# A four-layer graph network: layer 1's row vector spread by one transfer, and the buffers divided anew

## The chip, the cores and the metric

The kernel runs on one core of a Trainium2 chip. Its engines are TensorE (PE, with its weight loads shown apart as PEld), VectorE (DVE), ScalarE (ACT), GpSimd (POOL) and SyncE (SP), which here only issues transfers. The metric is device time in microseconds of the whole program; less is better. A line number such as L911 is a line of the kernel before the change.

## The reference

There are 32 independent graphs of 512 nodes with 256 features, each with a dense 512 x 512 adjacency matrix, all in 32-bit floats. Four layers follow each other, each with a residual and a layer norm:

```
x = norm(x + MLP(adj @ x + (1 + eps) x))            # layer 0, hidden 512
x = norm(x + GAT(x, adj > 0.5))                     # layer 1, 4 heads of 64
x = norm(x + MHA(x, log(adj + 1e-6)))               # layer 2, 8 heads of 32
x = norm(x + softmax(mask((x W) x^T * adj)) x)      # layer 3
```

The change touches layer 1. There the score of the pair (i, j) in head h is leaky_relu(dst[i, h] + src[j, h]) with slope 0.2, masked by adj > 0.5, and goes through a softmax over j.

## The kernel before

The graphs are not worked off one after another. The function `graph` describes all work of one graph as named steps, each with an engine, a cost in microseconds, the steps that it follows, and the buffers that it takes. `Plan.order` then simulates all engines with these costs and writes the instructions of all graphs in the order in which its simulation started them. Up to six graphs are open at once (the `window`), so that layers of different graphs overlap. Each engine works off its instructions in that order; the planner's times decide the order alone, and the real engines wait on semaphores. The tuple given to `plan.run` holds the due time between graphs (33.0), how far ahead of the earliest candidate it may look (0.0), the window, the price put on a change of TensorE's tiling mode (55.0), and seeds that move the due times of some steps at random; a search over seeds is what "annealed" means.

`transfer(name, us, after, queue)` stands for a transfer that was issued: `us` on a modelled queue, which works off its entries one at a time, and then a fixed 2.0 us until it has landed.

Memory is divided in classes. "B" are large buffers of 8 KB a partition (a 512 x 512 matrix), "C" those of 4 KB, and "D" strips of 2 KB (128 x 512). A take such as `D=A00/8` needs more than 8 free ones of the class. Strips hold the adjacency rows A0 of layer 0 and A3 of layer 3, ATd, layer 3's z3 and eT, the nodes' masks, and some rows of layers 1 and 2. Large buffers hold the transposed adjacency AT, h1T, layer 1's four z and layer 2's E chunks.

Layer 1 writes the exponential of the leaky score as a product, so that most of it needs no exponential of a matrix. The row vector R holds, for each of the four heads, exp(0.8 src[j]) over the 512 nodes; S and T hold factors that depend on i or j alone by partition. One activation (L911) makes Relu(S R - T) for 128 x 512 pairs, and VectorE (L922) adds T and multiplies by the edge mask. For L911 a head's R, one row of 512, must stand in all 128 partitions. It is made as columns, transposed by TensorE (step Rt, L853), copied to SBUF as rows of 128 (Re, L858), stored to a scratch tensor in device memory (Rsi, L863), and read back with one row spread over all partitions (Rl0 to Rl3, L872), one head after the other. Two more rows, the sums xs of the features over all nodes, go the same way: they are spread into the strip xsr (hsbi, L880), and VectorE multiplies them by the weights into hs (hsl, L888), a bias needed by layer 1's output copy (L959). GpSimd issues transfers that add while they move: the biases onto x (L583), and sums of z (L974 in layer 1, L1149 in layer 2), on a queue of their own.

Of the kernel before, what the change touches and what calls it, by code (L numbers as in the profile page):

```python
# [10 lines left out]
F32 = mybir.dt.float32  # L11
I32 = mybir.dt.int32
U8 = mybir.dt.uint8
AF = mybir.ActivationFunctionType
# [3 lines left out]
P = 128  # L18
# [6 lines left out]
H1 = 4  # L25
# [5 lines left out]
def row_bcast(ap, n):  # L31

    return bass.AP(tensor=ap.tensor, offset=ap.offset, ap=[[0, P], [1, n]])
# [13 lines left out]
class Plan:  # L47
# [30 lines left out]
    def step(self, name, eng, us, after=(), take=(), free=(), mode=""):  # L78


        def add(emit):
            steps = self.steps[-1]
            known = {**steps, **{f"^{n}": s for n, s in self.steps[0].items()}}
            assert name not in steps and all(a in known for a in after), (name, after)
            takes = []
            for b in take:
                kind, _, key = b.partition("=")
                key, _, rest = key.partition("/")
                takes.append((kind, key or kind, int(rest or 0)))
            steps[name] = Step(eng, us, dict.fromkeys(after), takes, mode, emit)  # L90
            for b in free:
                self.free(b, (name,))
            return emit

        return add
# [129 lines left out]
def fast_path(  # L225
# [23 lines left out]
    nc = tc.nc  # L249
    B, N, D = x.shape  # L250
    NC = N // P
    DC = D // P
# [10 lines left out]
    dram = ctx.enter_context(tc.tile_pool(name="dram", bufs=3, space=bass.MemoryType.DRAM))  # L263
# [33 lines left out]
    def blk(i):  # L297
# [1 line left out]


    plan = Plan({
        "B": 11, "C": 12, "D": 19, "p": 8,

        "live": 6, "L0": 1, "L1": 2, "L2": 2, "L3": 1, "AT": 4, "zs": 7, "edge": 1, "tmp": 2,
    })
    step = plan.step

    def prev(name, i):

        return (f"{name}{i-1}",) if i else ()  # L310

    def row(name, n):
        return tuple(f"{name}{i}" for i in range(n))

    def transfer(name, us, after, queue="q1"):


        @step(f"{name}.q", queue, us, after)
        def _():
            pass  # L320

        @step(name, None, 2.0, (f"{name}.q",))
        def _():
            pass
# [231 lines left out]
    def graph(g):  # L556
# [3 lines left out]
        t = {"g": g}  # L560

        def big(key, shape, name):
            return sb.tile(shape, F32, tag=f"B{slot[key]}", name=f"{name}_{g}")
# [4 lines left out]
        def strip(key, shape, name):  # L568
            return sb.tile(shape, F32, tag=f"D{slot[key]}", name=f"{name}_{g}")
# [88 lines left out]
        for c in range(NC):  # L658

            @step(  # L660
                f"la{c}i", "sp", 0.45, (f"la{c-1}i",) if c else (),
                take=(f"D=A0{c}/5",) if c else ("live", "L0", "D=A00/8"),
            )
            def _(c=c):
                t[f"A{c}"] = strip(f"A0{c}", [P, N], f"A{c}")
                nc.sync.dma_start(t[f"A{c}"], adj[g].rearrange("(c p) m -> p c m", p=P)[:, c, :])
# [192 lines left out]

        @step("Rsi", "sp", 0.45, ("Re",))  # L860
        def _():
            t["Rdram"] = dram.tile([H1 * NC + DC, P], F32, tag="R_dram", name=f"R_dram_{g}")
            nc.sync.dma_start(t["Rdram"], t["Rr"])  # L863

        transfer("Rs", 0.2, ("Rsi",))

        for h in range(H1):

            @step(f"Rl{h}i", "sp", 0.45, ("Rs",) + ((f"Rl{h-1}i",) if h else ()), take=(f"D=R{h}/4",))
            def _(h=h):  # L870
                t[f"R{h}"] = strip(f"R{h}", [P, N], f"R_bc_{h}")
                nc.sync.dma_start(t[f"R{h}"], row_bcast(t["Rdram"][h * NC : (h + 1) * NC, :], N))  # L872

            transfer(f"Rl{h}", 0.8, (f"Rl{h}i",))


        @step("hsbi", "sp", 0.45, ("Rs",), take=("D=xsr/3",))
        def _():
            t["xsr"] = strip("xsr", [P, 2, D], "xs_row")
            nc.sync.dma_start(t["xsr"][:, 0, :], row_bcast(t["Rdram"][H1 * NC :, :], D))  # L880

        transfer("hsb", 0.4, ("hsbi",))

        @step("hsl", "dve", 0.7, ("hsb", "^weg"), free=("xsr",))
        def _():
# [18 lines left out]
        for h in range(H1):  # L904
            for c in range(NC):

                @step(f"z{h}{c}", "act", 0.7, (f"Rl{h}", "ST") + prev(f"z{h}", c), take=() if c else (f"B=z{h}",))
                def _(h=h, c=c):
                    if c == 0:
                        t[f"e{h}"] = big(f"z{h}", [P, NC, N], f"z1_{h}")  # L910
                    nc.scalar.activation(  # L911
                        t[f"e{h}"][:, c, :], t[f"R{h}"], AF.Relu,
                        bias=t["nT"][:, h, c : c + 1], scale=t["S"][:, h, c : c + 1],
                    )

            for k in range(2):

                @step(f"zm{h}{k}", "dve", 1.32, (f"z{h}{2*k+1}",) + row("ed", NC))
                def _(h=h, k=k):
                    for c in (2 * k, 2 * k + 1):  # L920
                        z = t[f"e{h}"][:, c, :]
                        nc.vector.scalar_tensor_tensor(  # L922
                            z, z, t["T"][:, h, c : c + 1], t["edge"][:, c, :], op0=ALU.add, op1=ALU.mult
                        )

        plan.free("edge", tuple(f"zm{h}{k}" for h in range(H1) for k in range(2)))
        for h in range(H1):
            plan.free(f"R{h}", row(f"z{h}", NC))


        for hp in range(H1 // 2):
# [484 lines left out]
    for g in range(B):  # L1416
        graph(g)
    with tc.manual_schedule():
        plan.run([(33, 0.0, 6, 55.0, ((619770, 10.0), (518002, 10.0), (122525, 2.0), (401816, 5.0), (736052, 5.0), (898543, 5.0), (151957, 2.0), (89616, 2.0), (541939, 5.0), (120127, 10.0), (238703, 2.0), (316405, 2.0), (831071, 5.0), (164665, 2.0)), (0.7, 0.0, 0.0))])

# [427 lines left out]
@with_exitstack  # L1850
def four_layer_graph_kernel(ctx: ExitStack, tc: tile.TileContext, *args):
    flags = ctx.enter_context(tc.tile_pool(name="flags", bufs=1))
    beyond = flags.tile([1, 1], I32, name="beyond")
    fast_path(tc, *args, beyond)
    taken = tc.nc.values_load(beyond, min_val=0, max_val=1,
                              skip_runtime_bounds_check_because="is_lt gives 0 or 1")
    with tc.If(taken > 0):
        general_path(tc, *args)
# [34 lines left out]
```

## Time and profile before

| | |
|---|---|
| time, median of 3 | 3014.51 us (3012.42 to 3014.51) |
| span of the profiled run | 3008.2 us |
| granted TensorE clock | 0.996 |
| R_bc<-R_dram | 128 transfers of 256 KB |
| xs_row<-R_dram | 32 transfers of 128 KB |
| R_dram<-R_rows | 32 transfers of 9 KB |
| DMA queue q0 (GpSimd's) | 346.06 MB, 60.4% of 16 engines' span |
| DMA queue q1 (SyncE's) | 149.75 MB, 15.5% of 16 engines' span |

An engine's busy share is over the whole span. The matmuls are pipelined, so TensorE's busy time can contain lost time. A wait in square brackets at the end of a line of the order of time is idle time ahead of that instruction and what ended it. In the chain that ended last, each piece is what the next one waited for.

### The profile page before, as it was taken

To read this page: it belongs to the slowest core of one execution; us is meant where nothing else is said; L and a number is where in the kernel's file an instruction comes from. 1 tells how busy PE (TensorE), PEld (TensorE's weight loads), DVE (VectorE), ACT (ScalarE), POOL (GpSimd) and SP (SyncE) were. 2 spreads that over 40 slices of the span, in tenths; PEclk is the share of its full clock that TensorE was granted. 3 is DMA by queue.
4 is the path that set the end of the run, shared out by engine and by line. 5 is a ranking of instruction groups with operands and counts; after the bars stand their busy time and mean duration, and the time that the engine had idled before them with its cause. 6 is when DMAs were issued, how large, how long until landed. Compare 5 with 4: busy or idle time off the path is not lost.

```text
span 3008.2 us, 42752 instructions
## 1 busy us (share of the span) xinstructions
PE 2938.5 (98%) x15521; PEld 1687.7 (56%) x15521; DVE 2060.2 (68%) x4133; ACT 1928.2 (64%) x3818; POOL 626.8 (21%) x688
## 2 busy tenths in 40 slices
PE   8999999999999999999999999999999999999998
PEld 6546565565555565655656556555556565565544
DVE  3567767667667677676676766766767767667776
ACT  4666766666666667566676666665666766657664
POOL 1222212222122221222211222212222212222120
PEclk9999999999999999999999999999999999999999
DMA  6887787787787787877878777778778787786770
GB/s 175 179 173 171 166 188 161 167 177 156 173 176 168 164 173 166 191 159 160 182 149 192 163 167 175 163 167 186 164 165 168 163 191 157 166 179 143 163 171 15
DMA packets 180320, 498.89 MB, mean 166 GB/s; under 512 B 17980, under 2 KB 57736, under 8 KB 156296
## 3 DMA queue, kind: packets, MB, share of 16 engines
q0 software_dynamic: 77472, 346.06, 60.4%
q1 hardware_dynamic: 101648, 149.75, 15.5%
q8 instruction: 125, 2.05, 0.3%
q14 instruction: 91, 0.75, 0.1%
q10 hardware_dynamic: 984, 0.28, 0.0%
HBM read 183.25 MB, written 17.08 MB: 67 GB/s over the span
## 4 chain that ended last, share of the span: by engine, by line
PE 73%; DVE 10%; DMA 9%; ACT 5%; issue 2%; POOL 1%; SPq 0%; ACTq 0%; POOLq 0%; DVEq 0%
PE s L1317 8%; PE o_ps L1174 7%; PE s L1116 7%; PE y_ps L766 7%; PE o_ps L946 6%; DVE z L922 5%; PE o_ps L1371 5%; PE iT_ps L1303 4%; PE h1T_ps L747 4%; PE v_ps L815 4%; PE o2p_ps L1259 4%; ACT z L911 4%; PE v_ps L1097 4%; DMA xs_row<-R_dram 3%; DMA R_bc<-R_dram 3%; PE qT_ps L1079 2%
## 5 line engine op out<-in xcount | busy, mean ns | idle before, releaser
L1138 DVE SCALAR_TENSOR_TENSOR z<-AT,z 128x1024 f32<-128x1024 f32 x512 | 616.3, 1219 | 214.4 <-ACT z L1129 210.2
L1129 ACT ACTIVATE z<-s 128x512 f32<-128x512 f32 x1024 | 566.1, 602 | 126.9 <-PE s L1116 123.0
L911 ACT ACTIVATE z<-R_bc,nT,S 128x512 f32<-128x512 f32 x512 | 380.0, 809 | 181.7 <-DMA R_bc<-R_dram 181.6
L637 ACT ACTIVATE x<-x,shift,rstd 128x256 f32<-128x256 f32 x508 | 283.2, 592 | 127.9 <-DVE shift L627 127.8
L922 DVE SCALAR_TENSOR_TENSOR z<-z,T,edge 128x512 f32<-128x512 f32 x512 | 350.4, 746 | 10.7 <-ACT z L911 10.2
L1149 POOL DMA_DIRECT2D z<-z x186 | 165.9, 901 | 787.5 <-DVE z L1138 337.6
L1116 PE MATMUL s<-qT,kT 32*128 32x512 f32 x2048 | 313.3, 638 | 2.1 <-ACT qT L1085 2.1
L619 POOL TENSOR_TENSOR rstd<-ve,nhalf 128x4 f32<-128x4 f32 (+1 forms) x131 | 161.3, 1232 | 682.9 <-DVE ve L613 634.3
L974 POOL DMA_DIRECT2D z<-z x256 | 226.4, 953 | 300.1 <-DMA z<-z 183.4
L747 PE MATMUL h1T_ps<-hT,w_sb 128*128 128x512 f32 x512 | 243.0, 599 | 23.2 <-ACT hT L731 22.9
L946 PE MATMUL o_ps<-z,v 128*64 128x512 f32 x1024 | 244.9, 608 | 17.4 <-ACT z L1129 13.0
L1174 PE MATMUL o_ps<-z,v 128*32 128x512 f32 x2048 | 257.6, 600 | 3.8 <-DVE z L1138 3.8
L1223 DVE RECIPROCAL rdT<-rdT 128x256 f32<-128x256 f32 x128 | 219.2, 1735 | 54.0 <-ACT rdT L1216 53.8
L1371 PE MATMUL o_ps<-x,eT 128*128 128x256 f32 x1024 | 237.1, 380 | 0.0
L1317 PE MATMUL s<-xT,iT 128*128 128x512 f32 x512 | 236.4, 605 | 0.0
L766 PE MATMUL y_ps<-w_sb,h1T 128*128 128x256 f32 x1024 | 226.2, 379 | 0.0
L596 DVE BATCH_NORM_STATS2 st<-x 128x6 f32<-128x256 f32 x508 | 211.0, 415 | 8.3
L1116 PEld LDWEIGHTS s<-qT,kT 32*128 32x128 f32 x2048 | 103.6, 183 | 199.9 <-ACT z L1129 68.0
L724 PE MATMUL hT_ps<-AT,x 128*128 128x384 f32 (+2 forms) x768 | 208.8, 381 | 1.8 <-ACT AT L701 1.8
L766 PEld LDWEIGHTS y_ps<-w_sb,h1T 128*128 128x128 f32 x1024 | 194.3, 190 | 26.3
L583 POOL DMA_DIRECT2D x<-biases x96 | 86.0, 897 | 584.0 <-PE hT_ps L724 294.2
L1371 PEld LDWEIGHTS o_ps<-x,eT 128*128 128x128 f32 x1024 | 189.4, 190 | 31.5 <-ACT z L1129 0.8
(152 smaller groups left out, 4196.3 us busy)
## 6 DMA issues: line engine op xcount, KB each, us to landing
z<-z POOLq DMA_DIRECT2D x186, 1024.0 KB, 7.8
A<-in_adj_dram SPq DMA_DIRECT2D x256, 256.0 KB
z<-z POOLq DMA_DIRECT2D x128, 512.0 KB, 8.2
x<-biases POOLq DMA_DIRECT2D x96, 512.0 KB, 5.5
R_bc<-R_dram SPq DMA_DIRECT2D x128, 256.0 KB
z<-z POOLq DMA_DIRECT2D x128, 256.0 KB, 8.6
x<-in_x_dram SPq DMA_DIRECT2D x32, 512.0 KB
out_dram<-x SPq DMA_DIRECT2D x31, 512.0 KB
```

Source lines behind the costliest of these rows:

```text
L637: nc.scalar.activation(xn, xn, AF.Identity, bias=t[f"shift{n}"][:, c : c + 1], scale=t[f"rstd{n}"][:, c : c + 1],)
L747: nc.tensor.matmul(ph, w1_sb[:, d, blk(f)], t["hT"][:, d, :], start=(d == 0), stop=(d == DC - 1))
L766: nc.tensor.matmul(py[:, j, :], t["h1T"][:, f, blk(2 * c2 + j)], w2_sb[:, f, :], start=(f == 0), stop=(f == HC - 1),)
L911: nc.scalar.activation(t[f"e{h}"][:, c, :], t[f"R{h}"], AF.Relu, bias=t["nT"][:, h, c : c + 1], scale=t["S"][:, h, c : c + 1],)
L922: nc.vector.scalar_tensor_tensor(z, z, t["T"][:, h, c : c + 1], t["edge"][:, c, :], op0=ALU.add, op1=ALU.mult)
L946: nc.tensor.matmul(po[j * F1 : (j + 1) * F1, :], t["v"][:, c, h * F1 : (h + 1) * F1], t[f"e{h}"][:, c, :], start=(c == 0), stop=(c == NC - 1),
L1116: nc.tensor.matmul(pk, t["k"][hs, o, blk(c)], t["q"][hs, o, :], start=True, stop=True)
L1129: nc.scalar.activation(t[f"E{k}"][:, j, :], t[f"ps{k}{j}"], AF.Exp, scale=QSCALE)
L1138: nc.vector.scalar_tensor_tensor(z, t["AT"][:, c, None, :].to_broadcast([P, 2, N]), ADJ_EPS, z, op0=ALU.add, op1=ALU.mult,)
L1174: nc.tensor.matmul(t[f"n{o}"][32 * j : 32 * j + 32, :], t["v2"][:, c, o * P + F2 * j : o * P + F2 * (j + 1)], t[f"E{k}"][:, j, :], start=( ...
L1317: nc.tensor.matmul(pt, t["iT"][:, d, blk(c)], t["xT3"][:, d, :], start=(d == 0), stop=(d == DC - 1),)
L1371: nc.tensor.matmul(py, t[f"eT{c}"][:, blk(m)], t["x"][:, m, :], start=(m == 0), stop=(m == NC - 1),)
```

## The change

R's 16 rows are stored without the two rows of sums and read back in one transfer to all partitions, 2,048 elements a partition in one run, into a large buffer that is given back after the last z of all heads. The two rows of sums get a scratch tensor, a store and a load of their own, and the planner's costs for them become larger (3.5 for the store, on a modelled queue of its own, and 2.0 for the load). R no longer takes strips; the same memory is divided in 13 large buffers and 11 strips, in place of 11 and 19. The order is searched anew, with other parameters and seeds. The arithmetic is the same.

```diff
     plan = Plan({
-        "B": 11, "C": 12, "D": 19, "p": 8,
+        "B": 13, "C": 12, "D": 11, "p": 8,
...
         @step("Rsi", "sp", 0.45, ("Re",))
         def _():
-            t["Rdram"] = dram.tile([H1 * NC + DC, P], F32, tag="R_dram", name=f"R_dram_{g}")
-            nc.sync.dma_start(t["Rdram"], t["Rr"])
+            t["Rdram"] = dram.tile([H1 * NC, P], F32, tag="R_dram", name=f"R_dram_{g}")
+            nc.sync.dma_start(t["Rdram"], t["Rr"][: H1 * NC, :])

         transfer("Rs", 0.2, ("Rsi",))

-        for h in range(H1):
-
-            @step(f"Rl{h}i", "sp", 0.45, ("Rs",) + ((f"Rl{h-1}i",) if h else ()), take=(f"D=R{h}/4",))
-            def _(h=h):
-                t[f"R{h}"] = strip(f"R{h}", [P, N], f"R_bc_{h}")
-                nc.sync.dma_start(t[f"R{h}"], row_bcast(t["Rdram"][h * NC : (h + 1) * NC, :], N))
-
-            transfer(f"Rl{h}", 0.8, (f"Rl{h}i",))
-
-
-        @step("hsbi", "sp", 0.45, ("Rs",), take=("D=xsr/3",))
+        @step("Rli", "sp", 0.45, ("Rs",), take=("B=R/3",))
+        def _():
+            t["Rbc"] = big("R", [P, H1, N], "R_bc")
+            nc.sync.dma_start(
+                t["Rbc"].rearrange("p h n -> p (h n)"), row_bcast(t["Rdram"], H1 * N)
+            )
+
+        transfer("Rl", 2.5, ("Rli",))
+
+
+        @step("xsi", "sp", 0.45, ("Re",))
+        def _():
+            t["xsdram"] = dram.tile([DC, P], F32, tag="xs_dram", name=f"xs_dram_{g}")
+            nc.sync.dma_start(t["xsdram"], t["Rr"][H1 * NC :, :])
+
+        transfer("xs", 3.5, ("xsi",), "qx")
+
+        @step("hsbi", "sp", 0.45, ("xs",), take=("D=xsr/3",))
         def _():
             t["xsr"] = strip("xsr", [P, 2, D], "xs_row")
-            nc.sync.dma_start(t["xsr"][:, 0, :], row_bcast(t["Rdram"][H1 * NC :, :], D))
-
-        transfer("hsb", 0.4, ("hsbi",))
+            nc.sync.dma_start(t["xsr"][:, 0, :], row_bcast(t["xsdram"], D))
+
+        transfer("hsb", 2.0, ("hsbi",))
...
-                @step(f"z{h}{c}", "act", 0.7, (f"Rl{h}", "ST") + prev(f"z{h}", c), take=() if c else (f"B=z{h}",))
+                @step(f"z{h}{c}", "act", 0.7, ("Rl", "ST") + prev(f"z{h}", c), take=() if c else (f"B=z{h}",))
...
-                        t[f"e{h}"][:, c, :], t[f"R{h}"], AF.Relu,
+                        t[f"e{h}"][:, c, :], t["Rbc"][:, h, :], AF.Relu,
...
-        for h in range(H1):
-            plan.free(f"R{h}", row(f"z{h}", NC))
+        plan.free("R", tuple(f"z{h}{NC-1}" for h in range(H1)))
...
-        plan.run([(33, 0.0, 6, 55.0, ((619770, 10.0), ...), (0.7, 0.0, 0.0))])
+        plan.run([(26, 0.09, 6, 15.0, ((856337, 5.0), ...), (0.8, 0.0, 0.0))])
```

More of the change, by code (lines that the diff above doesn't have):

```diff
@@ L1418, in fast_path @@
     with tc.manual_schedule():
-        plan.run([(33, 0.0, 6, 55.0, ((619770, 10.0), (518002, 10.0), (122525, 2.0), (401816, 5.0), (736052, 5.0), (898543, 5.0), (151957, 2.0), (89616, 2.0), (541939, 5.0), (120127, 10.0), (238703, 2.0), (316405, 2.0), (831071, 5.0), (164665, 2.0)), (0.7, 0.0, 0.0))])
+        plan.run([(26, 0.09, 6, 15.0, ((856337, 5.0), (575719, 5.0), (896648, 2.0), (745051, 2.0), (644513, 5.0), (934653, 2.0), (193643, 2.0), (77466, 2.0), (498260, 5.0), (730218, 5.0), (783040, 2.0), (491194, 2.0)), (0.8, 0.0, 0.0))])
 @with_exitstack
```

## The prediction

> **What bounds the kernel now.** I read the page first (busy shares), then TensorE's waits, then the order of time of one period on each engine, then the chain that ended last. The page says that TensorE (PE) is the bound:
>
> ```profile
> PE 2938.5 (98%) x15521; PEld 1687.7 (56%) x15521; DVE 2060.2 (68%) x4133; ACT 1928.2 (64%) x3818; POOL 626.8 (21%) x688
> DMA packets 180320, 498.89 MB, mean 166 GB/s; under 512 B 17980, under 2 KB 57736, under 8 KB 156296
> ```
>
> The change leaves every matmul as it is, so only time that PE loses can be won. The chain shows the y matmuls of successive graphs starting at 290.90 and 2785.76 us, 27 periods apart: 92.4 us a period. The waits of PE alone show little of the loss (h1T for hT, 22.9 us in 24 times); the rest shows as stretches that last longer than the same work elsewhere. One period of PE in order of time (start, duration, line, work, count):
>
> ```profile
> 1003.26 1.02 PE L747 MATMUL h1T_ps<-hT,w_sb 128*128 128x512 f32 x2
> 1005.92 1.12 PE L747 MATMUL h1T_ps<-hT,w_sb 128*128 128x512 f32 x2 [1.63 <-ACT hT L731]
> 1006.88 1.88 PE L1079 MATMUL kT_ps<-xT,wkT 128*128 128x512 f32 x4
> 1008.60 1.88 PE L747 MATMUL h1T_ps<-hT,w_sb 128*128 128x512 f32 x4
> 1010.41 2.98 PE L1116 MATMUL s<-qT,kT 32*128 32x512 f32 x16
> 1013.32 3.99 PE L946 MATMUL o_ps<-z,v 128*64 128x512 f32 x16
> 1017.24 1.06 PE L1204 MATMUL d_ps<-z,ones 128*32 128x512 f32 x8
> ...
> 1040.13 1.14 PE L1116 MATMUL s<-qT,kT 32*128 32x512 f32 x8
> 1041.20 3.65 PE L946 MATMUL o_ps<-z,v 128*64 128x512 f32 x16
> 1044.78 1.14 PE L1116 MATMUL s<-qT,kT 32*128 32x512 f32 x8
> ```
>
> From start to start, four h1T matmuls take 1.81 us (1008.60 to 1010.41) but 3.62 us where they wait for hT: 1.8 lost. Sixteen s take 2.91 us, twice eight take 2.14: 0.8 lost. The first o_ps takes 3.92, the second 3.58: 0.3 lost. That is 2.9 us in this period; the next one, read in the same way (h1T 2.56, s 2.91, o_ps 3.96 us), loses 1.9. I take 2.4 us a period, or 74 us over 31 periods: all that a better order can bring in this place. It lies where ACT and DVE are late, and the chain says why:
>
> ```profile
> 1078.85 0.29 SPq L863 DMA_DIRECT2D R_dram<-R_rows  x1
> 1083.58 1.97 SPq L872 DMA_DIRECT2D R_bc<-R_dram  x4
> 1085.66 0.42 SPq L880 DMA_DIRECT2D xs_row<-R_dram  x1
> ```
>
> ```profile
> 1088.92 1.52 ACT L911 ACTIVATE z<-R_bc,nT,S 128x512 f32<-128x512 f32 x2 [5.88 <-DMA R_bc<-R_dram]
> ```
>
> ```profile
> 1091.51 0.43 DVE L888 CUSTOM_DVE_ANT_0 xs_row<-xs_row,wgT 128x256 f32<-128x256 f32 x1 [6.95 <-DMA xs_row<-R_dram]
> ```
>
> The rows end on DVE at 1078.83. The store is seen to land 4.7 us later, ACT then stands 5.88 us for the first strip and DVE 6.95 us for the sums, both with later work queued in order behind (hT's copy and kT's on ACT; ten z products and the last residual on DVE). Over the run these two are 181.6 us (37 times) and 209.2 us (28 times). From 300 to 2850 us the chain passes 16 times through xs_row and 14 times through R_bc as its long transfer: both must shorten before PE gains all.
>
> The planner did not expect these waits. By its costs the first z follows the rows by 0.13 + 0.45 + 0.05 + 0.2 + 2.0 + 0.45 + 0.05 + 0.8 + 2.0 = 6.1 us; the trace has 10.1. The sums' product, with 0.4 on the queue and at most four strips of 0.8 ahead of it, follows by 5.7 to 8.9 us; the trace has 12.7. So the orders on ACT and DVE are made for transfers about 4 us quicker than they are.
>
> [...] the store issued at 2831.10, outside heavy accumulation, lands in 1.27 us, the one at 1078.85 starts its packets 4 us after issue, when a z accumulation (8 KB pieces, about 0.64 us each) has just ended.
>
> ```profile
> 2831.10 1.27 DMA R_dram<-R_rows
> ```
>
> [...] iT after s takes 1.91 us (1048.83 to 1050.74) where four kT take 1.72, so 0.2 us a change.
>
> **The change, part by part.** *R as 16 rows, one spread.* It removes three issues a graph (the four take 1.97 us, so about 1.5 us of the sync queue) and moves the same 1 MB in 8 KB runs in place of 2 KB ones. The trace has no plain 8 KB read of this kind; bounds for it: the 2 KB packets take 0.097 us on average, so 8 descriptors of 8 KB at the same rate take 8 x 4 x 0.097 = 3.1 us an engine, and an accumulating 8 KB piece takes 0.66, so at most 5.3 us. I take the lower, a plain copy. But every z now waits for all four heads. All four strips were there between 1088.92 and 1091.5 (xs_row lay behind them), so the first z can move by -0.5 to +2.6 us; I take +1.1, that is 11.2 us after the rows. The store stays at 1.3 to 5 us with what is queued on the engines[...]. The plan now gives 0.13 + 0.45 + 0.05 + 0.2 + 2.0 + 0.45 + 0.05 + 2.5 + 2.0 = 7.8 us, so the lag on ACT falls only from 4.0 to 3.4 us.
>
> *Sums stored apart.* One more store and issue (0.3 us on a queue that is nearly idle, hidden). The load is no longer after four strips in the queue, at most after one spread; I leave its landing at 12.7 us, range 10 to 13. What changes is the plan: 0.13 + 0.45 + 0.05 + 3.5 + 2.0 + 0.45 + 0.05 + 2.0 + 2.0 = 10.6 us. The lag falls from at least 3.8 to about 2.1 us, so DVE should be given other work ahead of the product, and the 209 us should fall to some 60 to 90. Its z products still can't start before ACT's first pair, 1.5 us after ACT is released: about 1091.5 again. So ACT's 3.4 us of lag is what remains on the path, of 5 us that DVE had in the mean (3.8 to 6.95).
>
> *Buffers.* 11 large of 8 KB and 19 strips of 2 KB are 126 KB a partition, 13 and 11 as well. R holds one large buffer from its load to its last z, about 18 of 92 us, so the others gain one to two. Strips: four went to R for those 18 us, so 15 become 11 for the rest. A new adjacency asks for more than 8 free ones; it now holds four from 1086 to 1173 us. That must become later or alternate with layer 3, which needs node, four A3, and at least one z3 and eT.
>
> *Order.* New seeds, and a price of 15 in place of 55 on a change of mode. The eight s groups of a graph fill four banks each of eight, so most changes are forced.
>
> Sum: a lag of 5 us becomes 3.4, a third of 2.4 us = 0.8 a period, and 0.2 for the free large buffers: 1.0 x 31 = 31 us. Start and end stay. 3014.5 - 31 = 2983.5, say 2984.
>
> **Rivals.** (a) *Nearly all of the stall goes* (2.4 x 31 = 74): 2940. For it: the sums' wait is the larger and is now planned; against it: the ACT lag stays. (b) *Modes eat the gain*: four more isolated groups a graph cost 4 x 0.2 = 0.8 us, 25 us in all: 3009, within 0.2%. For it: the lower price; against it: bank limits set most changes. (c) *Strips become the wait*, slower: layer 3 with one z3 and one eT at a time runs a chain of 0.69 + 0.73 + 0.8 + 0.44 + 0.5 plus hops, about 4 us a chunk, against 1.72 + 0.44 + 1.73 = 3.9 us of PE. Any lateness of a load then lands on PE; 0.5 us on four chunks is 2 us, less the gain of 1.0, so +1.0 x 31 = 31: 3045. For it: PE today waits only 6.3 us for adjacency because loads are early; against it: the planner prices those loads at 2.0 each plus 2.0, 10 us for four, and the trace's four, issued at 1086.14, are through by about 1094. (d) *One spread blocks*: if it queues behind an accumulation with 5.3 us of its own, the first z comes 3 to 4 us later than now and the loss grows by 0.5 us a period: 3030.
>
> **How the numbers follow.** The forecast has 0.48, (a) 0.18, (b) 0.07, (c) 0.19, (d) 0.08. Faster 0.66, same 0.07, slower 0.27. The range runs from (a) to a little over (c): 2940 to 3048.
>
> **What would show it.** Right: the DVE wait for xs_row far under 209 us; the ACT wait for R_bc about as now (120 to 200 us, some 31 times); PE's h1T wait for hT under 15 us; a period near 91.4 us; R store packets still up to 4 us after issue. Wrong: TensorE waits on A or A3 loads or on ta (rival c), more groups of s alone (b), ACT waits for R_bc over 250 us (d), or a period at or above 92.4 us.

## The result, and the profile after

The changed kernel takes 3194.29 us (median, 3191.75 to 3204.05) against 3014.51 us: 1.0604 of the time before, with an interval of 1.0581 to 1.0627. It is 180 us slower where 31 us less were forecast, and far outside the range.

The page of the changed kernel, in the lines that answer to those of before:

```profile
PE 3010.2 (94%) x15521; PEld 1685.4 (53%) x15521; DVE 2034.3 (64%) x4133; ACT 1939.7 (61%) x3818; POOL 627.1 (20%) x688
DMA packets 166786, 498.90 MB, mean 156 GB/s; under 512 B 16732, under 2 KB 56488, under 8 KB 138664
```

The matmuls are the same 15521, and the bytes are the same. The profiled run is the longest of the four, so its span grew by more than the median did: from 3008.2 to 3202.2 us, by 194.0. TensorE's idle time (span less busy time) grew from 69.7 to 192.0 us, by 122; its busy time for the same matmuls grew from 2938.5 to 3010.2, by 72. These are two losses of different kinds, and both need a reason.

The idle time has names. TensorE's largest waits, first in the kernel before and then in the changed one (who waited for whom, total, times, longest):

```profile
PE h1T_ps L747 <- ACT hT L731: 22.9, 24, 2.2
PE o_ps L946 <- ACT z L1129: 13.0, 15, 2.1
```

```profile
PE s L1323 <- ACT iT L1315: 73.7, 40, 5.6
PE hT_ps L724 <- DMA x<-in_x_dram: 65.5, 17, 4.5
PE qT_ps L1085 <- ACT xT L1070: 7.3, 1, 7.3
```

Neither of the first two of the changed kernel stood among the waits before. The first is layer 3's s, which waits for ScalarE to copy iT; the second is layer 0's hT, which waits for the load of x. What lies behind them is read from the chain that ended last (start, duration, what):

```profile
1708.13 8.97 DMA out_dram<-x
1717.10 0.02 issue
1717.12 7.91 DMA x<-in_x_dram
1725.02 0.14 issue
1725.16 5.39 PE hT_ps L724 x20
...
1739.24 7.11 DMA R_dram<-R_rows
...
1746.48 6.11 DMA R_bc<-R_dram
...
1752.69 0.61 ACT z L918
...
1754.00 0.47 ACT iT L1315
...
1756.69 3.66 PE s L1323 x4
```

Two chains of transfers now end at TensorE, one 17 times and one 40 times. In the first, an output is stored, which frees a middle buffer; x of another graph is loaded into it, and its matmul stands ready. In the second, the row is stored and spread; ScalarE waits with z at the head of its queue, and iT's copy stands behind z. The load of x waited for an output's store in the kernel before too (27 times, against 26 now). What is new is its lead, the time from its issue to the first matmul that reads x:

```profile
1123.03 0.38 SPq L673 DMA_DIRECT2D x<-in_x_dram  x1
1177.22 0.38 PE L724 MATMUL hT_ps<-ATd,x 128*128 128x128 f32 x2
```

These two lines of the kernel before belong to one graph: 54 us, so nobody waited. Over the 32 graphs the median lead is 54 us in the kernel before and 8 us in the changed one.

The busy time has another reason, seen in the windows around such a wait (us, busy time and instructions of PE, PEld, DVE, ACT and POOL, then the granted clock, the DMA share and GB/s):

```profile
1547.40:1551.00 3.60, 3.60 (x17) 2.85 (x15) 0.00 (x0) 0.00 (x0) 0.92 (x1) 1.00 0.96 284
1551.00:1555.70 4.70, 0.02 (x2) 0.00 (x1) 0.00 (x0) 1.83 (x4) 0.00 (x0) 0.98 1.07 251
1555.70:1562.70 7.00, 6.91 (x8) 2.50 (x9) 3.60 (x9) 7.00 (x12) 0.00 (x0) 0.53 0.40 83
```

The same place in order of time, from the issue of the row's store on:

```profile
1536.51 0.33 SPq L863 DMA_DIRECT2D R_dram<-R_rows  x1
...
1553.87 0.81 ACT L918 ACTIVATE z<-R_bc,nT,S 128x512 f32<-128x512 f32 x1 [9.02 <-DMA R_bc<-R_dram]
...
1555.70 7.19 PE L1323 MATMUL s<-xT,iT 128*128 128x512 f32 x8 [4.68 <-ACT iT L1315]
...
1559.06 0.43 DVE L895 CUSTOM_DVE_ANT_0 xs_row<-xs_row,wgT 128x256 f32<-128x256 f32 x1 [15.70 <-DMA xs_row<-xs_dram]
...
1562.73 1.04 PE L1066 MATMUL xT_t<-ident,x 128*128 128x128 f32 x8
```

The same work in the kernel before:

```profile
1061.49 5.42 PE L1317 MATMUL s<-xT,iT 128*128 128x512 f32 x12
1066.74 0.27 PE L1023 MATMUL y_t<-ident,yT 128*128 128x128 f32 x1
```

TensorE waits 4.7 us for iT, and the 7 us that follow run at 0.53 of the clock: eight s take 7.03 us from start to start, where twelve took 5.25 in the kernel before. The mean clock is 0.972 against 0.996, which is 0.028 x 3202 = 90 us against 0.004 x 3008 = 12: 78 us more, about the 72 by which the busy time grew.

### The profile page after: what moved, and what is told of

It is laid out like the page before. It is cut to its first block, busy times and chain, and to the rows that moved or that the text cites. A ratio compares the mean times of both kernels' runs of the same rounds, so it can differ in the third digit from the quotient of the medians.

```text
span 3202.2 us, 42943 instructions
## 1 busy us (share of the span) xinstructions
PE 3010.2 (94%) x15521; PEld 1685.4 (53%) x15521; DVE 2034.3 (64%) x4133; ACT 1939.7 (61%) x3818; POOL 627.1 (20%) x688
## 4 chain that ended last, share of the span: by engine, by line
PE 69%; DMA 21%; ACT 5%; DVE 2%; issue 1%; POOL 0%; ACTq 0%; SPq 0%; POOLq 0%; DVEq 0%
PE hT_ps L724 8%; PE o_ps L1377 7%; DMA R_bc<-R_dram 7%; PE s L1323 7%; PE s L1122 6%; PE o_ps L952 6%; PE o_ps L1180 6%; DMA R_dram<-R_rows 4%; DMA x<-in_x_dram 4%; DMA out_dram<-x 4%; PE o2p_ps L1265 4%; PE v_ps L1103 3%; PE y_ps L766 3%; PE kT_ps L1085 3%; PE qT_ps L1085 3%; PE h1T_ps L747 2%
## 5 line engine op out<-in xcount | busy, mean ns | idle before, releaser
L1135 ACT ACTIVATE z<-s 128x512 f32<-128x512 f32 x1024 | 563.7, 603 | 98.9 <-PE s L1122 97.4
L918 ACT ACTIVATE z<-R_bc,nT,S 128x512 f32<-128x512 f32 x512 | 375.9, 809 | 198.6 <-DMA R_bc<-R_dram 198.6
L1323 PE MATMUL s<-xT,iT 128*128 128x512 f32 x512 | 281.2, 680 | 74.4 <-ACT iT L1315 73.7
L637 ACT ACTIVATE x<-x,shift,rstd 128x256 f32<-128x256 f32 x508 | 292.0, 596 | 48.2 <-DVE shift L627 48.0
L1122 PE MATMUL s<-qT,kT 32*128 32x512 f32 x2048 | 295.4, 641 | 0.8 <-DVE R_rows L858 0.5
L1377 PE MATMUL o_ps<-x,eT 128*128 128x256 f32 x1024 | 250.2, 388 | 1.3 <-ACT eT L1367 1.3
L747 PE MATMUL h1T_ps<-hT,w_sb 128*128 128x512 f32 x512 | 233.2, 598 | 0.3 <-DVE rd L1022 0.3
L724 PE MATMUL hT_ps<-AT,x 128*128 128x384 f32 (+2 forms) x768 | 228.7, 410 | 1.2 <-ACT AT L701 1.2
L1229 DVE RECIPROCAL rdT<-rdT 128x256 f32<-128x256 f32 x128 | 212.2, 1713 | 16.0 <-ACT rdT L1222 15.8
L895 DVE CUSTOM_DVE_ANT_0 xs_row<-xs_row,wgT 128x256 f32<-128x256 f32 x64 | 27.2, 424 | 298.0 <-DMA xs_row<-xs_dram 296.8
L1323 PEld LDWEIGHTS s<-xT,iT 128*128 128x128 f32 x512 | 101.8, 214 | 211.1 <-ACT iT L1315 115.0
```

The costliest lines, as they stand in the source:

```text
L724: nc.tensor.matmul(ph[:, cols], t["x"][:, m, blk(d)], moving, start=(k == 0), stop=(k == len(parts) - 1),)
L747: nc.tensor.matmul(ph, w1_sb[:, d, blk(f)], t["hT"][:, d, :], start=(d == 0), stop=(d == DC - 1))
L918: nc.scalar.activation(t[f"e{h}"][:, c, :], t["Rbc"][:, h, :], AF.Relu, bias=t["nT"][:, h, c : c + 1], scale=t["S"][:, h, c : c + 1],)
L1122: nc.tensor.matmul(pk, t["k"][hs, o, blk(c)], t["q"][hs, o, :], start=True, stop=True)
L1135: nc.scalar.activation(t[f"E{k}"][:, j, :], t[f"ps{k}{j}"], AF.Exp, scale=QSCALE)
L1323: nc.tensor.matmul(pt, t["iT"][:, d, blk(c)], t["xT3"][:, d, :], start=(d == 0), stop=(d == DC - 1),)
```

## The experiments

Two theories. **O**: the new order is at fault, because the planner believes that every transfer of SyncE lands 2.0 us after its time on the queue, and the search puts work where transfers are still on their way. **R**: the new transfers are at fault, because the row arrives later than before. All ratios are to the kernel before; an interval follows each.

**e1 and e2: the new order with the old transfers.** e1 goes back to one store of 18 rows and four spreads, e2 only to four spreads:

```diff
-            nc.sync.dma_start(
-                t["Rbc"].rearrange("p h n -> p (h n)"), row_bcast(t["Rdram"], H1 * N)
-            )
+            for h in range(H1):
+                nc.sync.dma_start(
+                    t["Rbc"][:, h, :], row_bcast(t["Rdram"][h * NC : (h + 1) * NC, :], N)
+                )
```

> The changed kernel with its order and buffers kept, but the transfers as they were before: one store of 18 rows, R spread by four transfers (a head's z waits for its own quarter), the sums read from the same scratch tensor. Theory O (the order is at fault: x is loaded too close to its first matmul and iT's copy stands behind z on ScalarE): within 1.5% of the changed kernel, 3150 to 3230 us, with the waits of TensorE for x and for iT still there. Theory R (the new transfers are at fault, the row arrives later): most of the 180 us comes back, 3010 to 3080 us.

> The changed kernel, only the spread of R cut in four transfers of 2 KB runs into the same large buffer. Theory R, if the wait for all four heads is the harm: ScalarE's wait for R_bc falls from 199 us to under 120 us and the time to under 3130 us. Theory O: 3170 to 3220 us.

Measured: e1 3240.77 us (ratio 1.0750, 1.0719 to 1.0782), e2 3250.34 us (1.0782, 1.0707 to 1.0857). Both are slower than the changed kernel: in this order the one spread is worth some 50 us, and undoing the change's transfers brings nothing back. e1 missed O's range by 11 us and e2 by 30, on the far side from R. TensorE's wait for x stays (65.0 us in e1), as O has it; a wait for xT's copy behind z joins it (41.6 us in e1, 50.1 in e2), and ScalarE's wait for R_bc is 231 us in e2, not less. Whether the sums are stored apart or not is not told apart here, since the intervals overlap.

The row is late in this order with either kind of transfer. From the store's issue to the first z, the median over the 32 graphs is 9.9 us in the kernel before, 13.9 in the changed one and 12.8 in e1. In e1 ScalarE then waits for the later heads' rows as well: 52 waits for R_bc in place of 31, and 16.3 us from the first z of a graph to its last in place of 14.0.

**e3, e4, e6: each wait taken away alone, and both.** In e3 and e6, z and the sums' product read constant tiles; the row and the sums are left out of layer 1, while their transfers still run:

```diff
-                        t[f"e{h}"][:, c, :], t["Rbc"][:, h, :], AF.Relu,
+                        t[f"e{h}"][:, c, :], w1_sb[:, 0, :], AF.Relu,
...
-                    t["xsr"][:, 1, :], t["xsr"][:, 0, :], wgT[:, o, :], TINY, 0.0,
+                    t["hsx"], wgT[:, o, :], wgT[:, o, :], TINY, 0.0,
```

In e4 and e6 only the output of the last graph is stored; the other 31 are left out:

```diff
+                if last:
+                    nc.sync.dma_start(out[g] ...)
-                nc.sync.dma_start(out[g] ...)
```

> The changed kernel with the row's transfers still made, but z and the sums' product read constant tiles in place of R and of the sums, so that nothing waits for them; this leaves R and the sums out of layer 1. Theory R: nearly all of the loss goes, 3000 to 3060 us. Theory O: TensorE's wait for iT (73.7 us, and part of 115 us before weight loads) goes with its slow clock windows, the wait for x stays: 3080 to 3130 us.

> The changed kernel without the stores of the output of the first 31 graphs, so that the load of x need not wait for the store that frees its buffer; the output of those graphs is left out. Theory O: the wait of hT for x (65.5 us) goes and with it about half of the half-speed clock windows (some 35 us): 3080 to 3110 us. Theory R: no change beyond the 3% of DMA traffic that is gone, 3170 to 3200 us.

> The changed kernel with both waits taken away (constants for R and the sums, no stores of the first 31 outputs). If the two waits are separate causes, their gains add: 3194 - 136 - 67 = 2991 us, 2980 to 3005. If both were one stall seen twice: 3040 to 3060 us, as with the row alone.

Measured: e3 3058.17 us (1.0145, 1.0076 to 1.0214), 136 us less than the changed kernel; e4 3126.95 us (1.0373, 1.0343 to 1.0403), 67 us less; e6 2958.90 us (0.9812, 0.9789 to 0.9835), 235 us less. TensorE's largest waits in e3:

```profile
PE hT_ps L724 <- DMA x<-in_x_dram: 64.7, 17, 4.6
PE AT_t L691 <- DMA A<-in_adj_dram: 4.9, 1, 4.9
```

and in e4:

```profile
PE s L1323 <- ACT iT L1315: 82.3, 52, 3.0
PE qT_ps L1085 <- ACT xT L1070: 7.0, 1, 7.0
PE hT_ps L724 <- DMA x<-in_x_dram: 6.4, 2, 4.8
```

Each edit takes away its own wait and leaves the other, so they are two causes; together they give 32 us more than the sum, so e6 fell below its expected band. The clock goes with them: its mean is 0.986 in e3, 0.980 in e4 and 0.998 in e6. e3 lands where R was expected, e4 a little above what O expected; neither theory is whole. What e3 shows is that in this order the row's lateness costs more than the wait for x; by e1 and e2, the old transfers do not cure it. e4 also takes away 3% of the bytes moved, and what that alone is worth was not tried.

**e5: what the row's wait costs in the old order.** The same edit as in e3, in the kernel before, with the same left out.

> The kernel before, where z and the sums' product read constant tiles, so that nothing waits for R or the sums (both left out of layer 1, the transfers still made). It measures what the wait for the row is worth in the old order; the prediction put it at 74 us. If that holds: 2935 to 2950 us. If the old order hides the row nearly whole: 2990 to 3015 us. In the new order the same edit gave 136 us.

Measured: 2920.71 us (0.9686, 0.9663 to 0.9708). The row's wait is worth 94 us in the old order and 136 in the new one. TensorE is then busy 99% of the span:

```profile
PE 2892.4 (99%) x15521; PEld 1675.3 (57%) x15521; DVE 2068.8 (71%) x4133; ACT 1943.0 (67%) x3818; POOL 628.1 (22%) x688
```

e6, with the waits gone from the new order too, is still 38 us behind e5, and most of this is busy time, 2923.0 against 2892.4 us, at a clock of 0.998 and 0.997. One difference between the two orders fits it. Counted along the matmuls of the traces, TensorE changes its tiling mode 855 times in the new order and 696 times in the old one: 159 more, which at the 0.2 us that the prediction read for a change are an estimated 32 us. No run changes their number alone.

**e7: the old order with the new transfers.** The order is that of the kernel before, step by step. The row's one spread is issued where the first of the four was, into a buffer of 8 KB of its own; the sums are stored apart; the other strips rotate over 15 slots, which this order never exceeds.

```diff
                 if h == 0:
+                    t["Rbc"] = sb.tile([P, H1, N], F32, tag="R_bc", name=f"R_bc_{g}")
+                    nc.sync.dma_start(
+                        t["Rbc"].rearrange("p h n -> p (h n)"), row_bcast(t["Rdram"], H1 * N)
+                    )
-                t[f"R{h}"] = strip(f"R{h}", [P, N], f"R_bc_{h}")
-                nc.sync.dma_start(t[f"R{h}"], row_bcast(t["Rdram"][h * NC : (h + 1) * NC, :], N))
```

> The kernel before in its own order, with the changed transfers alone: 16 rows stored, one spread into a buffer of 8 KB apart, the sums stored and loaded apart, the other strips 15. Theory O (the order made the loss, the transfers are no worse): 2995 to 3025 us. Theory R (a later row is harmful in any order): 3040 to 3100 us.

Measured: 3069.80 us (1.0181, 1.0160 to 1.0201), so R holds in the old order: 55 us lost. A period in order of time (SyncE's issues, then ScalarE's first z):

```profile
1100.14 0.33 SPq L875 DMA_DIRECT2D R_dram<-R_rows  x1
1100.81 0.79 SPq L877 DMA_DIRECT2D xs_dram<-R_rows  x1
1106.13 0.34 SPq L887 DMA_DIRECT2D R_bc<-R_dram  x1
```

```profile
1112.13 1.52 ACT L928 ACTIVATE z<-R_bc,nT,S 128x512 f32<-128x512 f32 x2 [7.81 <-DMA R_bc<-R_dram]
```

From the store's issue to the first z pass 12.0 us, where the kernel before took 10.1 (1078.85 to 1088.92), 1.9 us more. Not all of it is the one spread: from the store's issue to that of the spread, which waits for it, it is 6.0 us here and 4.7 there, so the store is no quicker for its 16 rows. Over the 32 graphs the median goes from 9.9 to 12.2 us, 0.8 of it up to the issue of the spread and 1.5 from there to the first z. Over the run ScalarE's wait for R_bc rises from 181.6 to 246.8 us, and TensorE's h1T, whose hT copy stands behind z, waits 73.0 us in place of 22.9. The clock falls from 0.996 to 0.985. e1 and e7 together part the two things that the change mixes: the new order with the old transfers loses 226 us, the old order with the new ones 55, and both together 180.

**e8, e9, e12: other orders.** e9 is the changed kernel and e12 the kernel before, each with its own costs and seeds from another search. The order of e12 has about the planned length of the old one, and that of e9 about that of the changed kernel's. e8 is the changed kernel with longer landings for six transfers and seeds searched for these:

```diff
-        @step(name, None, 2.0, (f"{name}.q",))
+        @step(name, None, LAND.get(name.rstrip("0123456789"), 2.0), (f"{name}.q",))
...
+    LAND = {'Rs': 4.5, 'Rl': 4.5, 'xs': 3.0, 'hsb': 4.0, 'out': 6.0, 'lx': 5.5}
```

> The changed kernel, with the planner's landing times after the queue raised from 2.0 us to about what the trace shows (R store and spread 4.5, output store 6.0, load of x 5.5, sums 3.0 and 4.0), and seeds searched anew for these. Theory O: x is then loaded well ahead of its matmul and iT's copy no longer stands behind z; TensorE's waits for x and iT fall under 30 us together and the time to 2950 to 3030 us. If the buffers are the cause (11 strips, 12 middle buffers leave no room), the waits stay and the time is over 3100 us.

> The changed kernel with its own costs, another order from a search of mine for the same costs and buffers. If the loss is the bad luck of one order, another one should land elsewhere, some at or under 3060 us. If the costs (2.0 us for every landing) make every such order lean on transfers that arrive late, it is again over 3120 us, with TensorE waiting behind some transfer.

> The kernel before with its own costs (2.0 us for every landing), buffers and transfers, and another order from a search of mine for these. If 19 strips and a row in four strips are what protects the old order, it is close to it, 2990 to 3060 us. If any order searched with landings of 2.0 us leans on late transfers and the old one was merely a lucky one, it is at 3100 to 3250 us, as the two orders of the changed kernel are (3194 and 3184).

Measured: e8 3248.84 us (1.0771, 1.0747 to 1.0794), e9 3183.75 us (1.0565, 1.0539 to 1.0590), e12 3111.32 us (1.0325, 1.0294 to 1.0357). e8 missed, and shows how such an order fails:

```profile
DVE nonode L1288 <- DMA nm<-in_nodemask_dram: 228.3, 26, 10.3
ACT eT L1369 <- DVE nonode L1288: 180.4, 25, 8.5
PE o_ps L1379 <- ACT eT L1369: 163.4, 26, 7.8
```

The waits of TensorE for x and iT are gone, as O expected. In their place a chain of three engines waits for the node mask, a load that still had the old landing of 2.0 us; the chain that ended last shows it taking 13.7 to 16.0 us in most graphs. The search had moved the slack to the transfers that were called long, and away from one that was still called short. TensorE waits for yet other work of ScalarE in e9 (layer 2's d_ps for h1T 96.8 us and for xT 58.3) and in e12 (layer 3's eT_t for z 98.9 us). The chains that ended last show that this work, too, stands behind the row: in one period of e12 (from 1580.91) the store takes 6.7 us and the spread 4.2, then comes ScalarE's z of layer 1 and then what TensorE waits for; in one of e9 (from 1531.29) they take 4.4 and 9.2 us. e12 says that the kernel before was not safe by its make: another order of it, as good by the plan (2908.0 against 2906.3 us), is 97 us slower.

**e10 and e11: landings long for all of SyncE's transfers.** In the changed kernel (e10) and in the kernel before (e11), with seeds searched for these costs:

```diff
+    LAND = {'': 6.0, 'Rs': 4.5, 'Rl': 4.5, 'xs': 3.0, 'hsb': 4.0, 'ldn': 11.0}   # e10
+    LAND = {'': 6.0, 'Rs': 4.0, 'Rl': 4.0, 'hsb': 5.0, 'ldn': 11.0}              # e11
```

> The changed kernel with the planner's landing time after the queue at 6.0 us for all of SyncE's transfers (R store and spread 4.5, sums 3.0 and 4.0, node mask 11.0) and seeds searched anew. e8 made some transfers long and its order leaned on the node mask, which it still took for short. If that is the whole trouble, TensorE's waits fall and the time is 2990 to 3070 us. If 11 strips and 12 middle buffers leave no room to load early, it stays over 3080 us.

> The kernel before (19 strips, R in four strips) with the same longer landing times in the planner (R 4.0, sums 5.0, node mask 11.0, others 6.0) and seeds searched anew. If honest transfer times are what an order needs, it beats both kernels: 2930 to 2990 us, with TensorE's waits for ScalarE behind R nearly gone. If the old order owed its time to luck in the seeds, it is at 3010 to 3080 us.

Measured: e10 3002.20 us (0.9960, 0.9947 to 0.9972), e11 2943.11 us (0.9766, 0.9747 to 0.9786). e11 beats both kernels. TensorE's page line and its two largest waits in e11:

```profile
PE 2910.8 (99%) x15521; PEld 1674.0 (57%) x15521; DVE 2017.9 (69%) x4133; ACT 1923.4 (65%) x3818; POOL 640.9 (22%) x688
```

```profile
PE AT_t L693 <- DMA A<-in_adj_dram: 4.9, 1, 4.9
PE xT_t L1062 <- ACT x L639: 3.4, 4, 0.9
```

The first is at the start of the run. ScalarE's wait for R_bc is down to 7.3 us in e11 and 4.8 in e10. The planner gave e8 and e11 the same end to within 0.1 us; on the chip they are 306 us apart. How much is true of the landing times in the plan decides what its length is worth. The end that `Plan.order` gives each kernel, beside the median measured, shows it (us):

| | plan | measured | over the plan |
|---|---|---|---|
| before, landings of 2.0 | 2906.3 | 3014.5 | 108 |
| after, landings of 2.0 | 2921.7 | 3194.3 | 273 |
| e9, landings of 2.0 | 2917.0 | 3183.8 | 267 |
| e12, landings of 2.0 | 2908.0 | 3111.3 | 203 |
| e8, six landings long | 2919.3 | 3248.8 | 330 |
| e10, all landings long | 2983.5 | 3002.2 | 19 |
| e11, all landings long | 2919.3 | 2943.1 | 24 |

**e13 and e14: the transfers exchanged in these two orders**, to find what is left between e10 and e11. e13 is e11 with the edit of e7, e14 is e10 with that of e1.

> The order of e11 (2943 us) with the changed transfers alone: 16 rows stored, one spread into a buffer apart, sums stored apart, the other strips 15. If transfers matter only where an order leans on them, this stays within 0.5% of e11: 2930 to 2958 us. If the one spread makes the row later than 4 us of added allowance covers, as in the old order (55 us lost there), it is 2970 to 3010 us, and the transfers explain the gap of 59 us between e10 and e11.

> The order and buffers of e10 (3002 us) with the transfers of before (18 rows stored at once, four spreads into the same buffer). If the transfers explain the gap between e10 and e11, this falls to 2945 to 2970 us. If the division in 13 and 11 buffers explains it, it stays at 2990 to 3025 us.

Measured: e13 2959.61 us (0.9829, 0.9802 to 0.9855), e14 3008.07 us (0.9979, 0.9971 to 0.9986). The new transfers cost e11 some 16 us; in e10 they seem to save some 6, at the edge of the noise. e13 fell just above its first band. So most of the 59 us between e10 and e11 does not come from the transfers. It stands in the plan: its two ends are 64 us apart. In the profiled runs 45 us of the gap are TensorE's busy time (2956.0 against 2910.8) and 15 its idle time, and e10's order changes the tiling mode 1004 times, e11's 747 times; at 0.2 us a change, an estimated 51 us. Why the search found no order with fewer changes for e10 is open: it can be the division in 13 and 11 buffers, the price on a change (10 against 20), or the draw of the search. These were not tried apart.

## Why the prediction was wrong

**The step that failed is the order**, which the prediction put as "New seeds, and a price of 15 in place of 55 on a change of mode", and costed by forced mode changes alone, with "Start and end stay" and all other waits as before. Every transfer that was hidden before was taken to stay hidden. That was no property of the kernel: the x load was issued 54 us ahead in one order and waited for in the other. What the new order did to TensorE was measured as two waits, 73.7 us for iT and 65.5 for x, and what e3, e4 and e6 give back is 136, 67 and 235 us. Under the old landing costs two orders of the changed kernel came out at 3194 and 3184 us, and a second one of the kernel before at 3111: of these four, the order of before is the best by far.

Two signs of it stood in the plan, before any run. By its own costs the new order ends at 2921.7 us, after the 2906.3 of the old one; the two are not priced alike, since the row and the sums now cost more, but a gain of 31 us does not stand there. And it sets the load of x a median of 8 us ahead of its first matmul, where the old one had 64.

**The bound** was read rightly: only what TensorE loses can be won, and the row's late arrival is the largest loss in the kernel before. Its size was off: the prediction had 74 us, e5 measured 94.

**The lag on ScalarE** was mis-sized in the sum. The first z was to move by +1.1 us, with a range up to +2.6; in the old order (e7) it moves by +2.3 in the median, and this costs 55 us, where the prediction booked the shortened lag as a gain. Rival (d) had the direction, but 3030 us, where e7 has 3070. In the changed kernel the first z comes 13.9 us after the store's issue in the median, in place of the 11.2 estimated. ScalarE's wait for R_bc, 198.6 us in all, stayed within the 120 to 200 named as a sign of being right: the sum does not say what stands behind it. The period above is one of its long ones: 17.4 us, of which the chain gives 5.9 to the store and 11.2 to the spread, for which the prediction had set 5.3 as the upper bound.

**The sums** were to make VectorE wait 60 to 90 us; it waits 296.8 (28 times). That the plan calls them later did not help, since they are later still: at 1559.06 in the period shown, 22.6 us after the store's issue, and 18.5 in the median, not 12.7.

**The store** was put at 1.3 to 5 us. Its 16 rows in place of 18 don't shorten it where accumulating transfers run (in the median their queue kept 0.91 of the 16 engines' time busy meanwhile in the kernel before, and all of it in the changed one): from its issue to that of the spread, which waits for it, the median is 4.9 us before and 7.0 in the changed kernel, and with the 18 rows of before in the new order (e1) 7.2. So the order made it longer.

**Strips** were the feared rival (c), and did not come: the waits for adjacency are 7.2 us. The buffers that the late x loads wait for are the middle ones, 12 in both kernels, and the prediction looked at no class but those whose number changed. But the room was not what made the lead short: with the same buffers e10 loads x a median of 28 us ahead.

**Modes**, rival (b), came in the background: 159 more changes of tiling mode, where the prediction took most of them as forced. Its 25 us fit the 31 us of busy time between e5 and e6, but they are hidden in the changed kernel under the waits and the clock.

**The clock** was missing altogether. In the clock records of the trace, all 27 idle stretches of TensorE of 3.5 us or more in the changed kernel (3.6 to 7.3 us) come with 3.4 or 6.8 us at half clock, which begin in them or at most 1.0 us after. That is up to an estimated 1.7 or 3.4 us lost on top of the wait, which is mostly 3.9 to 4.7 us long, so such a wait costs up to nearly twice its length. Shorter ones came with the same, though not always: all five of 2.1 to 3.6 us in the kernel before, two of the three of 2.5 to 3.3 us in the changed one, and in e7, where no wait for hT is longer than 2.2 us, 20 of the 30 of 2.0 to 2.5 us. What length of wait is enough is not shown. The kernel before had only five idle stretches of 2 us or more, the changed one has 30; so the price of a wait in the first was no measure for the waits in the second.

## What to carry to other kernels

An order that a search makes from a model of costs can spend all slack that the model grants; here the transfers priced too short were the ones waited for, and repairing some of the prices moved the wait to the next (e8). Price every transfer by its landing under load, all of them at once, before searching, and read from the trace how far ahead of its use each load is issued: that lead, not the absence of a wait, says what a new order may keep. Compare plan and chip first: here every order that ran 100 us or more over its plan had landings priced too short. And try new transfers in the old order and old ones in the new (e1, e7) before reading a time that changed with both.

## What the runs showed of the hardware

- How long a transfer of SyncE took to land depended in these runs on what else moved at the time more than on its size. The row's store of 8 or 9 KB took 1.27 us with GpSimd's accumulating queue idle (2831.10 in the kernel before). In the medians of 32 graphs, up to the issue of the spread, it took 1.5 us in e10, where that queue kept 0.3 of the 16 engines' time busy meanwhile, and 7.0 us in the changed kernel, where it kept all of it busy. The number of rows made no such difference: 18 rows 1.4 us in e14 and 7.2 in e1, 16 rows 1.5 in e10 and 7.0 in e2. A 512 KB load or store of x took 7.8 to 9.4 us in the chain after, the spread mask of 256 KB 13.7 to 16.0 in the chain of e8.
- The packets of the one spread of 1 MB, in runs of 8 KB, were hardly quicker for their size than those of 2 KB: in the packet records of the changed kernel an 8 KB packet of it takes 0.31 us (median) and a 2 KB packet of the same queue 0.084, nearly the same rate; an accumulating packet of 8 KB takes 0.64. In e2's order the four spreads cost some 50 us more than the one, while in e11's order the changed transfers cost 16 us more than the old ones; what decides between the two is not shown.
- Each of the 27 idle stretches of 3.6 to 7.3 us on TensorE in the changed kernel came with 3.4 or 6.8 us at half clock, in the clock records of the trace, and those of 2.0 to 2.5 us did so in 20 of 30 cases in e7. Of the 194 us by which the span grew, some 70 are the slower clock: 72 us more busy time for the same matmuls, at a mean clock of 0.972 in place of 0.996.
